# Second cross attention of a decoder: the next sequence's keys go ahead of a step's scores

## The chip, the cores and the metric

The kernel runs on one core of a Trainium2 chip. The metric is the device time of one execution in microseconds (us), as a median over runs. The engines are TensorE (PE for matmuls, PEld for its weight loads), VectorE (DVE), ScalarE (ACT), GpSimd (POOL) and SyncE (SP), which here issues DMAs. Each engine works through its own instructions in order; semaphores tie the engines together.

## The reference, cut to what matters

The kernel computes a whole decoder of two layers on 16 sequences of 100 rows and 256 columns: retention, a cross attention, a mixture of experts, a Mamba block, a second cross attention and a product in int8, each with a residual and a layer norm. The change is in the second cross attention, which has 16 heads of 64 columns and a context of 361 rows and 192 columns for each sequence:

```python
q = (x @ Wq).reshape(B, Nq, h, dh)
k = (context @ Wk).reshape(B, Nk, h, dh)
v = (context @ Wv).reshape(B, Nk, h, dh)
scores = jnp.einsum('bqhd,bkhd->bhqk', q, k) * scale
attn = jax.nn.softmax(scores, axis=-1)
out = jnp.einsum('bhqk,bkhd->bqhd', attn, v).reshape(B, Nq, h * dh)
return out @ Wo + bo
```

All data are float32 but the int8 product at the end, which is done in bf16.

## The kernel before, in words

The second cross attention is `cross1`, and its loop is `attend`, which serves nothing else. The order of TensorE, ScalarE and VectorE in it is the order in which the code is written (`manual_schedule`); POOL and SP are left to the framework. The work goes in steps, numbered n from 0. Step n belongs to sequence b = n // 4 and to four of its 16 heads, quad = n % 4. There are 64 such steps and two more that only end the pipeline. A step has these parts:

- `scores(b, quad)`: four matmuls (L1656, each over 64 rows, two heads side by side on the array) into two tiles `sc`; two maxima on VectorE (L1661, tile `top`); four exponentials on ScalarE (L1666), each with its sum, into `s` and `den`.
- `prepare(b + 1, quad)`: for the next sequence, a list of one or two pieces. The first, `keys`, makes two key tiles: two matmuls over 128 rows of the context (L591) and two over the remaining 64 (L593, side by side), and two copies on VectorE (L1620, tile `k`). The second, `sources`, makes a third of the values in the same way (L591, L593, copies at L1637, tile `v`). It is missing at quad 0. At quad 0 `prepare` also issues the load of the context on SP (L581). The last sequence has nothing to prepare, so the list is empty in steps 60 to 63.
- `values(b', quad')` for the step two earlier (`depth` is 2): first the transposes of the weights' first two column blocks (L600), with the copies to `pT` by VectorE for the first block and by ScalarE for the second (L603); then, as its second piece, the transposes of the third block, its copy by ScalarE, twelve products with the values (L1695) and a copy to `oT` by ScalarE (L1701).
- `weigh`: the reciprocal of the sums on VectorE (L1674) and a multiplication of the four heads' weights by it on POOL (L1675).
- After the last quad of a sequence `finish`: the output projection (L155) and a row sum on VectorE (L1712). After quad 2 of every fourth sequence `queries` for the next four. `later` holds the pieces of the layer norm (means with a square root on ScalarE, L192; normalization, L200) and of the int8 product (L1785 to L1839), one or a few at the end of certain steps.

PSUM holds three tags of tiles with two buffers each: `sc` for scores (two banks a tile), `mm` for keys, values and the projections, `tr` for transposes and the products. A step with all its parts takes four tiles of `tr`: the two first transposes, the third, and the products, so the third waits for VectorE's copy of the first, and the products wait for ScalarE's copy of the second.

Of the kernel before, what the change touches and what calls it, by code (L numbers as in the profile page):

```python
# [90 lines left out]
class Net:  # L91
# [452 lines left out]
    def attend(self, scores, prepare, values, finish, queries, weigh, depth, later):  # L544

        n_quads = 4 * B
        engines = {mybir.EngineType.PE, mybir.EngineType.Activation, mybir.EngineType.DVE}  # L550
        with self.tc.manual_schedule(engines=engines):
            queries(0)
            for part in range(4):
                for step in prepare(0, part):
                    step()
            for n in range(max(n_quads + depth, max(later) + 1)):
                b, quad = divmod(n, 4)
                ahead, behind = [], []
                if n < n_quads:
                    scores(b, quad)  # L560
                    if b + 1 < B:
                        ahead = prepare(b + 1, quad)
                if depth <= n < n_quads + depth:
                    behind = values(*divmod(n - depth, 4))
                for i in range(max(len(ahead), len(behind))):
                    for steps in (ahead, behind):
                        if i < len(steps):
                            steps[i]()
                if n < n_quads:
                    weigh(b, quad)  # L570
                if n < n_quads and quad == 2 and b % G == G - 1 and b + 1 < B:
                    queries(b // G + 1)
                if depth <= n < n_quads + depth and (n - depth) % 4 == 3:
                    finish((n - depth) // 4)
                for step in later.get(n, []):
                    step()
# [1448 lines left out]
```

## Time and profile before

| what | value |
|---|---|
| time, median of 3 runs | 2023.19 us (2020.81 to 2028.84) |
| the profiled execution's own time | 2028.71 us |
| its span, first to last instruction | 2026.5 us |
| busy TensorE, share of the span | 1815.4 us, 90% |
| busy VectorE | 1134.7 us, 56% |
| busy ScalarE | 975.7 us, 48% |
| busy POOL | 683.5 us, 34% |
| mean granted TensorE clock | 0.942 of full speed |
| the first scores of the second cross attention | 1333.8 us |
| the first scores of step 60, the first without keys | 1957.65 us |

The profile is of one execution. Its rows give an instruction's start, its duration, the line that issued it and the tiles that it writes and reads; "idle before" names the time that the engine had nothing to run and what ended it. The granted clock is given by window: 1.00 is full speed, 0.50 is half. A group of matmuls in float32 shows two records for each matmul. The steps of the loop are told apart by their scores (L1656).

### The profile page before, as it was taken

Reading aid. Unit: us, or ns where it says so; the run is one execution under the profiler, and the core shown is the slowest. Engines: PE = TensorE matmul, PEld = TensorE weight load, DVE = VectorE, ACT = ScalarE, POOL = GpSimd, SP = SyncE. Lnnn points to the kernel's source line nnn. Section 1 sums busy time; section 2 is a strip of 40 time slices with the busy share of each in tenths; the row PEclk is TensorE's granted clock in tenths of the full one; section 3 lists DMA queues with packets and bytes.
Section 4 is the critical chain, followed back from the end, with each engine's and each line's share of the span. In section 5 each row is a group of like instructions: output and inputs, shape, how many; then the busy total and the mean of one; then the engine's idle time right before and its main releaser. Section 6 shows DMA issues by size and latency. Waiting matters only on the chain. (4 is left out here: it accounts for less than half of the span.)

```text
span 2026.5 us, 31942 instructions
## 1 busy us (share of the span) xinstructions
PE 1815.4 (90%) x12268; PEld 1071.4 (53%) x12268; DVE 1134.7 (56%) x2466; ACT 975.7 (48%) x2293; POOL 683.5 (34%) x501
## 2 busy tenths in 40 slices
PE   6998899999949996789898898999999999999985
PEld 3566556556535664455455455545555555555554
DVE  2454576767742222687888867444436545444654
ACT  4553376666622221487676676423334434344343
POOL 1322232334330001457557566422222322322231
PEclk8999999989869998899898899999999999999996
DMA  4700600001023111422111111000000000000000
GB/s 133 320 1 1 213 30 24 27 22 40 3 96 131 45 45 38 129 92 77 42 43 60 40 51 46 20 15 9 8 8 8 16 16 8 8 16 9 8 9 8
DMA packets 46848, 96.98 MB, mean 48 GB/s; under 512 B 5844, under 2 KB 25940, under 8 KB 44266
## 3 DMA queue, kind: packets, MB, share of 16 engines
q1 hardware_dynamic: 41642, 83.75, 12.3%
q0 software_dynamic: 5056, 11.20, 1.8%
q8 instruction: 98, 1.61, 0.3%
q14 instruction: 52, 0.43, 0.1%
HBM read 69.48 MB, written 25.44 MB: 47 GB/s over the span
## 5 line engine op out<-in xcount | busy, mean ns | idle before, releaser
L1675 POOL TENSOR_TENSOR s<-s,den 100x1444 f32<-100x1444 f32 x64 | 166.1, 2595 | 506.3 <-DVE den L1674 465.7
L155 PE MATMUL mm<-xT,w_mamba_in 128*128 128x400 f32 x512 | 206.7, 548 | 28.6 <-ACT sz L1353 22.7
L1666 ACT ACTIVATE s<-sc,top 100x361 f32<-100x361 f32 x256 | 140.4, 561 | 182.5 <-DVE top L1661 174.6
L603 ACT COPY pT<-tr 128x400 f32<-128x400 f32 (+1 forms) x192 | 94.1, 494 | 187.7 <-PE tr L600 185.9
L1204 DVE SCALAR_TENSOR_TENSOR xc<-mm,pv,xc 128x388 f32<-128x388 f32 (+2 forms) x192 | 119.9, 625 | 76.7 <-ACT xc L1199 69.2
L737 POOL TENSOR_SCALAR w_experts<-w_experts 100x1444 f32<-100x1444 f32 x64 | 89.0, 1390 | 217.8 <-DVE w_experts L733 171.5
L155 PEld LDWEIGHTS mm<-xT,w_mamba_in 128*128 128x128 f32 x512 | 101.2, 207 | 115.1 <-ACT sz L1353 30.6
L745 ACT ACTIVATE w_experts<-w_experts,top 100x361 f32<-100x361 f32 x256 | 149.3, 586 | 22.5 <-POOL w_experts L737 22.4
L1661 DVE TENSOR_REDUCE top<-sc 100x2 f32<-100x722 f32 x128 | 110.1, 901 | 87.0 <-PE sc L1656 87.0
L603 DVE COPY pT<-tr 128x400 f32<-128x400 f32 x192 | 105.4, 568 | 58.3 <-PE tr L600 51.4
L733 DVE TENSOR_SCALAR_CACHE_REDUCE w_experts<-sc 100x361 f32<-100x361 f32 x256 | 121.2, 530 | 16.2 <-PE sc L727 15.6
L600 PEld LDWEIGHTS tr<-cn,s 100*128 100x128 f32 (+1 forms) x768 | 76.1, 154 | 87.2 <-issue 63.9
L1637 DVE COPY v<-mm 128x512 f32<-128x512 f32 (+1 forms) x96 | 61.9, 686 | 107.3 <-PE mm L593 107.3
L155 PE MATMUL sc<-w_experts,e_xT 128*128 x256 | 117.1, 601 | 2.1 <-DMA e_x<-rows 2.1
L1387 POOL TENSOR_TENSOR y<-y,sz 128x400 f32<-128x400 f32 x64 | 66.5, 1040 | 145.1 <-DVE y L1384 112.3
L600 PE MATMUL tr<-cn,s 100*128 100x100 f32 (+1 forms) x768 | 99.3, 267 | 17.2 <-DVE pT L603 17.0
L600 PE MATMUL tr<-cn,w_experts 100*128 100x100 f32 (+1 forms) x768 | 97.8, 267 | 13.7 <-ACT w_experts L745 6.6
L1695 PE MATMUL tr<-pT,v 128*64 128x100 f32 (+1 forms) x1536 | 98.2, 268 | 12.1 <-ACT pT L603 7.3
L1324 POOL TENSOR_TENSOR L<-L,cols 100x800 f32<-100x800 f32 x64 | 100.0, 1563 | 23.6 <-DMA L<-sums 23.5
L1407 PE MATMUL acc<-y,w_mamba_out 128*128 128x400 f32 x256 | 102.3, 523 | 3.7 <-ACT w_mamba_out L1414 1.9
L1620 DVE COPY k<-mm 128x361 f32<-128x361 f32 x128 | 62.3, 529 | 68.1 <-PE mm L593 68.1
L591 PE MATMUL mm<-ctx,x_wk 128*128 128x361 f32 x256 | 95.3, 494 | 2.2 <-DVE v L1637 1.6
(298 smaller groups left out, 3647.5 us busy)
## 6 DMA issues: line engine op xcount, KB each, us to landing
L<-sums SPq DMA_DIRECT2D x64, 312.5 KB
rows<-nothing SPq DMA_DIRECT2D x15, 1024.0 KB
w_experts<-in_moe_w_dram SPq DMA_DIRECT2D x24, 512.0 KB
ctx<-in_ctxT_dram SPq DMA_DIRECT2D x32, 361.0 KB
e_x<-rows SPq DMA_DIRECT2D x32, 128.0 KB
rows<-e_y SPq DMA_DIRECT2D x32, 128.0 KB
w_mamba_in<-in_m_w_in_dram SPq DMA_DIRECT2D x1, 2048.0 KB
w_mamba_in<-in_m_w_in_dram POOLq DMA_DIRECT2D x1, 2048.0 KB
```

The lines of the kernel that those rows point to most:

```text
L155: self.nc.tensor.matmul(out, lhsT, rhs, start=i == 0, stop=i == len(pairs) - 1)
L600: self.nc.tensor.transpose(pt[:n, h * T : (h + 1) * T], probs[:, h, k0 : k0 + n], self.ident(T))
L603: evict(pT[:n, k, :], pt[:n, :GT])
L733: nc.vector.tensor_scalar(s[:, h, :], sc[h // 2][:T, h % 2, :CTX], -1e4, 1e4, ALU.max, ALU.min, accum_out=top[:, h : h + 1],)
L745: nc.scalar.activation(s[:, h, :], s[:, h, :], AF.Exp, bias=top[:, h : h + 1], scale=-1.0, accum_out=dens[b][:, hd : hd + 1],)
L1204: nc.vector.scalar_tensor_tensor(a3[:, :, s:], p3[:, :, : T - s], w(k), a3[:, :, s:], ALU.mult, ALU.add)
L1324: nc.gpsimd.tensor_tensor(ls[n], ls[n], bc(c, 3, T), ALU.subtract)
L1407: nc.tensor.matmul(acc[:, c, :GT], self.w_out[:, i, c * P : (c + 1) * P], y, start=i == 0, stop=i == 15)
L1661: nc.vector.tensor_reduce(top[:, 2 * p : 2 * p + 2], sc[p][:T, :, :CTX], AX.X, ALU.max, negate=True)
L1666: nc.scalar.activation(s[:, h, :], sc[h // 2][:T, h % 2, :CTX], AF.Exp, bias=top[:, h : h + 1], accum_out=den[:, h : h + 1],)
L1675: nc.gpsimd.tensor_tensor(s, s, bc(den, 2, CTX), ALU.mult)
L1695: nc.tensor.matmul(po[64 * jj : 64 * jj + 64, i * T : (i + 1) * T], v[k][:n, (4 * quad + h) * 64 : (4 * quad + h + 1) * 64], pT[:n, k, h * ...
```

## The change

In a step of `attend`, the first piece of `prepare` (the keys of the next sequence) is taken from its list and issued ahead of the scores. In the loop that interleaves what is left, the pieces of `values` are now named before those of `prepare`. A step thus runs: keys, scores, first transposes, values, then third transposes and products; before it ran: scores, keys, first transposes, values, third transposes and products.

```diff
                 b, quad = divmod(n, 4)
                 ahead, behind = [], []
                 if n < n_quads:
-                    scores(b, quad)
                     if b + 1 < B:
                         ahead = prepare(b + 1, quad)
+                        ahead.pop(0)()
+                    scores(b, quad)
                 if depth <= n < n_quads + depth:
                     behind = values(*divmod(n - depth, 4))
                 for i in range(max(len(ahead), len(behind))):
-                    for steps in (ahead, behind):
+                    for steps in (behind, ahead):
                         if i < len(steps):
                             steps[i]()
```

## The prediction

> **What bounds the kernel now.** I read the page first, then the waits of the second cross attention (1333 us to the end), then the timeline of single steps, then TensorE's busy time and granted clock in short windows.
>
> ```profile
> span 2026.5 us, 31942 instructions
> ...
> PE 1815.4 (90%) x12268; PEld 1071.4 (53%) x12268; DVE 1134.7 (56%) x2466; ACT 975.7 (48%) x2293; POOL 683.5 (34%) x501
> ...
> PEclk8999999989869998899898899999999999999996
> ```
>
> TensorE is the bound; in the stage concerned, slices 27 to 39, its clock is nearly whole. The waits of that stage (us in total, times, longest) leave little on TensorE itself:
>
> ```profile
> PE tr L600 <- DVE pT L603: 17.0, 18, 1.8
> ...
> PE tr L1695 <- ACT pT L603: 7.3, 6, 2.3
> ```
>
> The stage makes 64 steps, numbered n from 0; n mod 4 = 0 begins a sequence and has keys but no values ("short step"). A short step, n = 32 (columns: start, busy, engine, line):
>
> ```profile
> 1666.43 1.46 PE L1656 MATMUL sc<-k,q 64*100 64x361 f32 x8
> ...
> 1667.83 1.48 PE L591 MATMUL mm<-ctx,x_wk 128*128 128x361 f32 x4
> ...
> 1670.05 0.91 PE L600 MATMUL tr<-cn,s 100*128 100x100 f32 x8
> 1670.14 0.98 DVE L1620 COPY k<-mm 128x361 f32<-128x361 f32 x2 [1.08 <-PE mm L593]
> ...
> 1671.04 0.56 DVE L603 COPY pT<-tr 128x400 f32<-128x400 f32 x1
> 1671.04 0.49 ACT L603 COPY pT<-tr 128x400 f32<-128x400 f32 x1 [0.42 <-PE tr L600]
> ...
> 1671.65 0.61 PE L600 MATMUL tr<-cn,s 100*105 100x100 f32 x4 [0.70 <-DVE pT L603]
> ...
> 1673.69 1.46 PE L1656 MATMUL sc<-k,q 64*100 64x361 f32 x8
> ```
>
> It lasts 7.26 us, with 0.70 idle. The keys stand between the scores and the transposes, so the maxima and the exponentials run under them, and ScalarE is free when the transposes come. A step with values (n = 31, 1657.16 to 1666.43) lasts 9.27 without a gap on TensorE.
>
> **The change part by part.** It adds and removes no instruction. On ScalarE, POOL and SP the order stays exactly as it is, the context loads included (one is issued at 1664.54 and first used at 1705, so moving its call ahead of the scores changes nothing). On TensorE and VectorE, in steps 0 to 59, keys come before scores and key copies before the maxima. Transposes stood before values already. Steps 60 to 63 have no keys and stay.
>
> *One switch less.* Keys end with two 64-row matmuls (L593), scores are 64-row too. At the start of step 2 the trace has 64-row products running straight into scores:
>
> ```profile
> 1344.05 1.13 PE L593 MATMUL mm<-x_wv,ctx 64*128 64x512 f32 x4
> 1345.01 1.38 PE L1656 MATMUL sc<-k,q 64*100 64x361 f32 x8
> ```
>
> From L593 to the next group is 0.96 here and 1.06 where transposes follow (1641.98 to 1643.04). The scores take 1.31 here (keys follow at 1346.32) and 1.39 behind 128-row products (1657.16 to 1658.55). So 0.18 is saved wherever scores come to stand behind keys and TensorE is the bound: steps 3 to 59 less 14 short ones, 43 x 0.18 = -7.7 us.
>
> *The short steps lose their cover.* Scores now run straight into transposes. The nearest row is step 62, where before has that order:
>
> ```profile
> 1978.71 1.73 DVE L1661 TENSOR_REDUCE top<-sc 100x2 f32<-100x722 f32 x2 [0.37 <-PE sc L1656]
> ...
> 1979.71 0.56 ACT L1666 ACTIVATE s<-sc,top 100x361 f32<-100x361 f32 x1 [5.77 <-DVE top L1661]
> ...
> 1980.35 0.57 DVE L603 COPY pT<-tr 128x400 f32<-128x400 f32 x1
> ...
> 1980.97 0.61 PE L600 MATMUL tr<-cn,s 100*105 100x100 f32 x4 [0.87 <-DVE pT L603]
> ...
> 1981.87 0.90 ACT L603 COPY pT<-tr 128x400 f32<-128x400 f32 x2
> ...
> 1982.43 1.31 PE L1695 MATMUL tr<-pT,v 128*64 128x100 f32 x24 [0.85 <-ACT pT L603]
> ```
>
> Queued behind the exponentials on ScalarE is the second transpose's copy, and the products need the bank that it frees. Count from the start of the keys. Key copies start at 2.31 (1670.14 - 1667.83) and take 0.90: VectorE is free at 3.21. Maxima 1.64 (1980.35 - 1978.71): copy pT at 4.85; third transposes 0.62 later, 5.47. Exponentials start 1.00 behind the first maximum, 4.21; 2.16 later (1981.87 - 1979.71) the other pT copy, 6.37; products 0.56 later, 6.93; the next step 1.24 later (1983.67 - 1982.43), 8.17. Against 7.26 that is +0.91. The early copies of the keys don't help, since the maxima wait behind them. Steps 4, 8, 12, 16, 32, 48: 6 x 0.91. Steps 24, 40, 56 end with int8 products and save one switch: 3 x 0.73. Steps 20, 36, 52 already wait 1.83 behind a normalization: about 3 x 0.3. In 28 and 44 an ACT_TABLE_LOAD (1.28) comes ahead of the exponentials: products 8.21, end 9.45 against 7.68, 2 x 1.77. Sum +12.1.
>
> *Steps with values* hide the same chain: transposes 3.43, values 4.17, products 7.60, with the copy ready at 6.93, 0.67 to spare. A table load eats it in 19, 35, 51 (about +0.4 each). Keys that follow int8 products (25, 26 and likewise) wait for the second bank until two L1832 (0.88 together) are done: 6 x 0.43. The row sum behind `finish` (0.42) ends as the second key matmul wants its bank, paid by a switch saved there. Values that waited for key copies in before no longer do: -1. Filling the pipe in steps 0 to 2: +0.8. With small switches: +2.3. Where the trace is silent on these, I bound them by 0 and +5.
>
> Without the clock: -7.7 + 12.1 + 2.3 = +6.7 us.
>
> *The clock.* Windows of 3.41 us (columns after the window: length, PE, PEld, DVE, ACT, POOL busy, PEclk, DMA):
>
> ```profile
> 1708.65:1712.06 3.41, 1.58 (x14) 1.16 (x12) 3.11 (x7) 2.65 (x9) 0.00 (x0) 1.00 0.00 0
> 1712.06:1715.48 3.42, 3.42 (x30) 2.67 (x30) 3.32 (x5) 0.83 (x3) 2.60 (x1) 0.50 0.00 0
> 1879.33:1882.74 3.41, 2.22 (x14) 1.02 (x12) 3.41 (x8) 1.50 (x5) 0.00 (x0) 1.00 0.00 0
> 1882.74:1886.15 3.41, 2.72 (x34) 2.00 (x36) 3.08 (x5) 1.99 (x7) 2.20 (x1) 1.00 0.00 0
> ```
>
> Idle 1.83 of a window, and the next ran at half clock; idle 1.19, and it did not. In this stage drops followed 1.47 and more, none 1.31 and less: I take 1.4. The new short step has gaps of 1.13 and 0.84 (4.34 to 5.47, 6.09 to 6.93), 1.98 together. A window must start between 2.94 and 4.92 to hold 1.4 of it: 1.98/3.41 = 58%. Nine plain steps 5.2 drops, three at about 74% 2.2, two always: 9.4, less the 2 of before (after steps 20 and 36) = 7.4. One drop costs 1.1: steps 20 and 21 together take 22.92, 36 and 37 22.62, but 52 and 53, without a drop, 21.68. +8.1 us.
>
> Here a rule speaks otherwise. The Trainium skill, "TensorE: Matmul & The Clock Gate", Part 1, has the clock fall only after a whole idle window of about 3.4 us. By it no gap here counts, and the sum stays +6.7; by the rows it is +14.8. The rows decide.
>
> The sum stands on the profiled execution (2028.71 us, span 2026.5), which lies 5.5 above the median of the runs; I add it to the median: 2023.2 + 14.8 = 2038.0.
>
> **The rivals.** About 0.5%, 10 us, is what a measurement of this kernel can tell from no change.
> - *The clock stays up* (not slower): decided in the window that holds both gaps; if it takes more than 1.98 idle, or the gaps fall into two windows (as in step 62, which had no drop), only +6.7: 2029.9. For: step 62. Against: step 61, with gaps of 0.67 and 0.85, dropped. Chance 0.23.
> - *No switch is saved*, 128-column keys before 100-column scores costing as much as 128 rows do: +22.5, 2045.7. Against: the rows at 1344. Chance 0.13.
> - *ScalarE is late in steps with values too*: above 0.67 of added delay each 0.2 costs 9 us; about 2050. Chance 0.05.
> - *Faster*: copies come early enough that also the 0.70 of 14 short steps goes, -7.7 - 9.8: 2006. The chain above speaks against it. Chance 0.06.
>
> **How the numbers follow.** The main case has 0.53, its own range 2033 to 2043, a tenth of it under 10 us. Slower: 0.48 + 0.13 + 0.05 = 0.66. Same: 0.05 + 0.23 + 0.02 (from the last rival) = 0.30. Faster 0.04. The range 2027 to 2048 holds the main case, the first rival and most of the second.
>
> **What would show it.** Right: short steps of about 8.2 us with two waits, on DVE pT and on ACT pT, at L600 and L1695 (together near 30 us more than before); value steps of 9.09; some seven more windows at half clock, starting within the products of short steps. Wrong: value steps still 9.27 (no switch saved), or waits in them before L1695; short steps at 7.3 or less; a clock that stays whole.

## The result, and the profile after

The changed kernel takes 2042.47 us (median of 5 runs, 2040.11 to 2053.88) against 2023.35 before (5 runs, 2020.81 to 2028.84). The ratio over all runs is 1.0104 with a 95% interval from 1.0080 to 1.0127 (that of the two medians alone is 1.0094): slower by 16 to 26 us. The prediction had 2038.0 with a range from 2027 to 2048 and gave "slower" 0.66.

From the page after, the span, TensorE's busy time and the granted clock:

```profile
span 2038.1 us, 31942 instructions
...
PE 1806.9 (89%) x12268; PEld 1079.5 (53%) x12268; DVE 1132.4 (56%) x2466; ACT 969.1 (48%) x2293; POOL 682.5 (33%) x501
...
PEclk9999999999869997999998999999999999999996
```

The instructions are as many as before. TensorE's busy time over the whole span is 8.5 us less, but that lies ahead of the changed stage. The stage is looked at from the start of step 0 to that of step 60; the first row is before, the second after (length, busy time of PE, PEld, DVE, ACT and POOL, granted clock, and two figures for DMA):

```profile
1333.77:1957.65 623.88, 603.06 (x3815) 329.04 (x3811) 312.70 (x586) 243.75 (x708) 165.17 (x65) 0.99 0.04 11
1326.40:1969.34 642.94, 603.90 (x3813) 342.13 (x3813) 309.93 (x585) 237.75 (x708) 165.02 (x65) 0.97 0.04 10
```

The stage is 19.1 us longer. TensorE's busy time in it is nearly the same and its idle time 18.2 us more. This doesn't make waiting the whole cause: the changed order saves TensorE busy time, and a lower clock adds some, as is shown below. (All line numbers from 560 on are one higher than before: L1656 is now L1657, L600 is L601, L603 is L604, L1695 is L1696.) The waits from 1326 us on (us in total, times, longest):

```profile
PE tr L1696 <- ACT pT L604: 22.2, 21, 2.3
PE tr L601 <- DVE pT L604: 21.1, 18, 1.6
```

Before, the two stood at 7.3 and 17.0: 19.0 us more. The wait for ScalarE's copy, which six instances had before, now comes in 21. The short step n = 32, whole:

```profile
1666.41 1.48 PE L592 MATMUL mm<-ctx,x_wk 128*128 128x361 f32 x4
...
1667.82 0.88 PE L594 MATMUL mm<-ctx,x_wk 64*128 64x361 f32 x4
1668.53 1.38 PE L1657 MATMUL sc<-k,q 64*100 64x361 f32 x8
1668.73 0.97 DVE L1621 COPY k<-mm 128x361 f32<-128x361 f32 x2 [2.88 <-PE mm L594]
1669.62 1.72 DVE L1662 TENSOR_REDUCE top<-sc 100x2 f32<-100x722 f32 x2
1669.84 0.91 PE L601 MATMUL tr<-cn,s 100*128 100x100 f32 x8
1670.61 0.56 ACT L1667 ACTIVATE s<-sc,top 100x361 f32<-100x361 f32 x1 [3.76 <-DVE top L1662]
...
1671.25 0.56 DVE L604 COPY pT<-tr 128x400 f32<-128x400 f32 x1
...
1671.87 0.61 PE L601 MATMUL tr<-cn,s 100*105 100x100 f32 x4 [1.12 <-DVE pT L604]
...
1672.78 0.90 ACT L604 COPY pT<-tr 128x400 f32<-128x400 f32 x2
...
1673.33 1.31 PE L1696 MATMUL tr<-pT,v 128*64 128x100 f32 x24 [0.85 <-ACT pT L604]
1674.57 0.88 PE L592 MATMUL mm<-ctx,x_wk 128*128 128x361 f32 x2
```

Keys, scores and transposes follow each other without a gap, then TensorE waits twice: 1.12 us for VectorE, which first copied the keys and then made the maxima, and 0.85 us for ScalarE, which is still at the exponentials when the second transpose wants its copy. The step takes 8.16 us; it took 7.26. A step with values, n = 3, has no gap and shows the other side of the change:

```profile
1348.00 0.88 PE L594 MATMUL mm<-ctx,x_wk 64*128 64x361 f32 x4
1348.71 1.38 PE L1657 MATMUL sc<-k,q 64*100 64x361 f32 x8
1350.02 0.91 PE L601 MATMUL tr<-cn,s 100*128 100x100 f32 x8
```

The same groups of step 3 in before:

```profile
1354.24 1.46 PE L1656 MATMUL sc<-k,q 64*100 64x361 f32 x8
1355.63 1.48 PE L591 MATMUL mm<-ctx,x_wk 128*128 128x361 f32 x4
1357.04 0.88 PE L593 MATMUL mm<-ctx,x_wk 64*128 64x361 f32 x4
1357.85 0.91 PE L600 MATMUL tr<-cn,s 100*128 100x100 f32 x8
```

From the start of the keys' second part to that of the next group it is 0.71 now, with scores next, and was 0.81, with transposes next. From the start of the scores to the next group it is 1.31 and was 1.39. The whole step is 9.07 us; it was 9.27.

The third effect is in the clock. In these traces the clock changes only at whole multiples of 3.41 us from each other. Windows cut at these times (columns as above), the first pair from step 28 on, the second in step 32:

```profile
1617.80:1621.21 3.41, 1.28 (x18) 1.09 (x20) 1.07 (x3) 3.05 (x10) 0.76 (x1) 1.00 0.00 0
1621.21:1624.63 3.42, 3.42 (x19) 1.92 (x14) 2.96 (x4) 0.33 (x1) 1.84 (x1) 0.50 0.02 5
1669.00:1672.42 3.42, 2.30 (x19) 1.34 (x15) 2.82 (x5) 1.81 (x7) 0.00 (x0) 1.00 0.00 0
1672.42:1675.83 3.41, 2.56 (x29) 1.76 (x28) 0.18 (x1) 1.58 (x5) 2.51 (x1) 1.00 0.00 0
```

In step 28 both gaps fell into one window, TensorE was idle for 2.13 of it, and the next window ran at half clock. In step 32 the two gaps, 1.12 and 0.85, fell into different windows, and the clock stayed. In steps 0 to 60 there were 11 such drops with 12 half-clock windows; before had 2. That the spans differ by only 11.6 has another reason, shown by the last experiment.

### The profile page after: what moved, and what is told of

Read it like the earlier page. It is cut to its first block, busy times and chain, and to the rows that moved or that the text cites. A ratio compares the mean times of both kernels' runs of the same rounds, so it can differ in the third digit from the quotient of the medians.

```text
span 2038.1 us, 31942 instructions
## 1 busy us (share of the span) xinstructions
PE 1806.9 (89%) x12268; PEld 1079.5 (53%) x12268; DVE 1132.4 (56%) x2466; ACT 969.1 (48%) x2293; POOL 682.5 (33%) x501
## 5 line engine op out<-in xcount | busy, mean ns | idle before, releaser
L604 DVE COPY pT<-tr 128x400 f32<-128x400 f32 x192 | 105.3, 569 | 54.4 <-PE tr L601 46.7
L604 ACT COPY pT<-tr 128x400 f32<-128x400 f32 (+1 forms) x192 | 93.0, 499 | 81.2 <-PE tr L601 79.9
L1696 PE MATMUL tr<-pT,v 128*64 128x100 f32 (+1 forms) x1536 | 102.5, 281 | 25.8 <-ACT pT L604 22.2
L601 PEld LDWEIGHTS tr<-cn,s 100*128 100x128 f32 (+1 forms) x768 | 76.2, 154 | 92.5 <-issue 64.5
L601 PE MATMUL tr<-cn,s 100*128 100x100 f32 (+1 forms) x768 | 99.4, 267 | 21.3 <-DVE pT L604 21.1
L592 PE MATMUL mm<-ctx,x_wk 128*128 128x361 f32 x256 | 105.6, 530 | 4.5 <-DVE v L1638 3.1
L601 PE MATMUL tr<-cn,w_experts 100*128 100x100 f32 (+1 forms) x768 | 97.2, 267 | 13.8 <-ACT w_experts L746 6.1
```

The costliest lines, as they stand in the source:

```text
L592: self.nc.tensor.matmul(out, lhsT, rhs, start=True, stop=False)
L601: self.nc.tensor.transpose(pt[:n, h * T : (h + 1) * T], probs[:, h, k0 : k0 + n], self.ident(T))
L604: evict(pT[:n, k, :], pt[:n, :GT])
L1696: nc.tensor.matmul(po[64 * jj : 64 * jj + 64, i * T : (i + 1) * T], v[k][:n, (4 * quad + h) * 64 : (4 * quad + h + 1) * 64], pT[:n, k, h * ...
```

## The experiments

Theory: three effects, switches of row tiling (between groups over 128 rows of the array and groups over 64) saved in steps with values, cover lost in short steps (n mod 4 = 0), and a clock that falls because of the gaps. The rivals are that the order costs or gains alike in every kind of step, and that the clock has nothing to do with the gaps. "Steps 0 to 60" is always the time from the start of step 0 to that of step 60, 623.88 us in the profile of before shown above.

**Keys ahead in steps with values only, and in short steps only.**

```diff
-                    if b + 1 < B:
-                        ahead = prepare(b + 1, quad)
-                        ahead.pop(0)()
+                    ahead = prepare(b + 1, quad) if b + 1 < B else []
+                    first = quad > 0        # the other kernel: quad == 0
+                    if ahead and first:
+                        ahead.pop(0)()
                     scores(b, quad)
+                    if ahead and not first:
+                        ahead.pop(0)()
```

> Keys go ahead of the scores only in steps with values (n mod 4 > 0); short steps (n mod 4 = 0) keep the old order. Theory (two effects of opposite sign: a switch of row tiling saved in value steps, cover lost in short steps): value steps 9.07 us instead of 9.27, short steps 7.26 again, windows at half clock between steps 0 and 60 back to about 2; steps 0 to 60 about 5 us shorter than before (ratio about 0.9975). Rival (keys ahead of scores cost time wherever they stand): value steps no shorter and the ratio over 1.000.

> Keys go ahead of the scores only in the short steps. Theory: the whole loss sits there. Short steps 8.2 to 9.9 us, value steps 9.27 as before, about 11 windows at half clock; steps 0 to 60 about 22 to 25 us longer than before, so somewhat more than the changed kernel's 19.1 (ratio 1.011 to 1.013). Rival (loss spread over all steps): less than half of 19 us.

Measured: value steps alone 2012.37 us, ratio 0.9938 (0.9926 to 0.9950); steps 0 to 60 615.9 us, 8 shorter (10.5 shorter than in the second profile of before, at the end of this section). Value steps without other work take 9.07, short ones 7.26, and there are two half-clock windows. Short steps alone 2048.76 us, ratio 1.0130 (1.0113 to 1.0147); steps 0 to 60 650.4 us, 26.5 longer, with value steps at 9.27, undisturbed short ones at 8.16 and 11 half-clock windows. So the change is two changes: one half of it is a gain of about 0.6%, the other a loss of 1.3%, and the kernel as changed shows what is left. In the stage the two make -8.0 + 26.5 = 18.5, against 19.1. Both came out above what was expected: the gain was 8 for 5, the loss 26.5 for 22 to 25.

**TensorE kept busy in the gaps.**

```diff
+            short = quad == 2 and b < B - 2      # the values' side of a short step
+
+            def fill(cols):
+                if short:
+                    idle = self.ps("mm")
+                    nc.tensor.matmul(idle[:, :cols], wk[:, :P], wv[:, :cols], start=True, stop=True)
+
             def transposes(ks):
                 ...
+                fill(512 if 0 in ks else 361)
```

> The changed kernel, and in each of the 14 short steps two more matmuls whose result nobody reads, one of 512 columns behind the first transposes and one of 361 behind the third ones, so that TensorE is busy in the two waits. Theory (the waits leave a window idle for over 1.4 us, and the next runs at half clock): windows at half clock between steps 0 and 60 fall from 11 to 4 or less, plain short steps 8.2 to 8.4, steps 0 to 60 about 7 to 10 us longer than before instead of 19 (ratio 1.004 to 1.005). Rival (the clock falls for another reason, or costs nothing by itself): still about 11 windows, or a ratio of 1.010 or more since the extra matmuls only add work.

Measured: 2024.14 us, ratio 1.0004 (0.9995 to 1.0013). The stage and its short step n = 32 (L1690 is the filling):

```profile
1326.44:1951.77 625.33, 606.87 (x3869) 336.63 (x3869) 309.32 (x585) 237.46 (x708) 165.03 (x65) 1.00 0.04 11
```

```profile
1662.32 0.91 PE L601 MATMUL tr<-cn,s 100*128 100x100 f32 x8
1663.06 1.05 PE L1690 MATMUL mm<-x_wv,x_wk 128*128 128x512 f32 x2
1664.35 0.61 PE L601 MATMUL tr<-cn,s 100*105 100x100 f32 x4 [0.24 <-DVE pT L604]
1664.79 0.80 PE L1690 MATMUL mm<-x_wv,x_wk 128*128 128x361 f32 x2
1665.80 1.31 PE L1704 MATMUL tr<-pT,v 128*64 128x100 f32 x24 [0.21 <-ACT pT L604]
```

The granted clock of the stage is 1.00, with no window at half speed, and the 28 useless matmuls make it 17.6 us shorter than the changed kernel (642.94 against 625.33). The short step still takes 8.16 us, since the products come when ScalarE's copy does; only the clock is different. So the gaps cause the drops, and a window at half clock costs 17.6 / 12 = 1.47 us. The gain was above what was expected, because both the number of windows saved and their price had been set too low.

**What makes the scores start sooner.**

```diff
-        for out, (lhsT, rhs) in zip(outs, wide):
-            self.nc.tensor.matmul(out, lhsT, rhs, start=True, stop=False)
-        for out, (lhsT, rhs) in zip(outs, halves):
-            self.nc.tensor.matmul(out, lhsT, rhs, start=False, stop=True)
+        for n, pairs in enumerate((halves, wide) if halves_first else (wide, halves)):
+            for out, (lhsT, rhs) in zip(outs, pairs):
+                self.nc.tensor.matmul(out, lhsT, rhs, start=n == 0, stop=n == 1)
```

`halves_first` is set for the keys alone.

> The changed kernel, with the two parts of the keys exchanged: the two matmuls over the remaining 64 rows first, then the two over 128 rows. The order keys, scores, transposes stays; only the neighbour of the scores is now a 128-row matmul. Theory (value steps gain because 64-row keys run into 64-row scores without a switch): value steps such as 3, 11, 27, 43 and 59 go from 9.07 back to about 9.25. Rival (the gain comes from the order of keys and scores as such, by way of the copies that are ready earlier): they stay at 9.07.

Measured: steps 3, 11, 27, 43 and 59 take 9.25 us each. The scores of step 3:

```profile
1350.68 1.46 PE L1657 MATMUL sc<-k,q 64*100 64x361 f32 x8
1352.07 0.91 PE L600 MATMUL tr<-cn,s 100*128 100x100 f32 x8
```

They last 1.39 again with a 128-row neighbour, in the same order of keys and scores. The order of keys and scores is still the new one, so the gain is that of neighbours with the same row tiling. (This is one run, of 2057.91 us. It is longer for a further reason: the keys now begin with matmuls that want both `mm` banks, and behind an output projection the second of them waits for the row sum that frees its bank. Such steps take 9.86 instead of 9.18.)

**All three copies of a short step by VectorE**, in the changed kernel.

```diff
-                    self.probs_transposed(s, pT, k, nc.scalar.copy if k else nc.vector.tensor_copy)
+                    on_act = k > 0 and not (quad == 2 and b < B - 2)
+                    self.probs_transposed(s, pT, k, nc.scalar.copy if on_act else nc.vector.tensor_copy)
```

> The changed kernel; in the 14 short steps all three copies of transposes are made by VectorE, so that none of them queues behind the exponentials on ScalarE. Theory (of the two waits of a short step the second, at the products, is ScalarE's queue; the first, at the third transposes, is VectorE's and stays): the first wait stays at about 1.1 us, the second shrinks from 0.84 to about 0.4, plain short steps 7.6 to 7.8 us instead of 8.16, fewer windows at half clock; 5 to 12 us shorter than the changed kernel (ratio against before 1.004 to 1.008). Rival (the products wait for something else, the scores' bank or the weights): short steps stay near 8.2 and the ratio near 1.010.

Measured: 2018.26 us, ratio 0.9977 (0.9968 to 0.9987). Its short step n = 32 takes 7.58 us:

```profile
1660.48 1.04 DVE L604 COPY pT<-tr 128x400 f32<-128x400 f32 x2
...
1661.10 0.61 PE L601 MATMUL tr<-cn,s 100*105 100x100 f32 x4 [1.12 <-DVE pT L604]
...
1661.64 0.56 PE L1697 MATMUL tr<-pT,v 128*64 128x100 f32 x8
1661.75 0.57 DVE L604 COPY pT<-tr 105x400 f32<-105x400 f32 x1 [0.23 <-PE tr L601]
...
1662.37 0.91 PE L1697 MATMUL tr<-pT,v 105*64 105x100 f32 x16 [0.17 <-DVE pT L604]
```

The first wait is the same to the hundredth, the wait on ScalarE is gone, and a wait of 0.17 on VectorE has come: the second wait was ScalarE's queue. With smaller gaps the drops fall to 5, of one window each. The gain over the changed kernel, 19.2 us in steps 0 to 60, is more than was expected. By the price of 1.47 the seven windows less make 10.3 of it, an estimate; the rest is the shorter waits.

**A better version.** Two kernels keep the keys ahead in steps with values only, and also exchange the copies of the first two transposes between VectorE and ScalarE. One does this in all short steps, the other only in the nine that neither follow a normalization nor have a table load. The exchange in the second:

```diff
+                    swap = quad == 2 and b in (0, 1, 2, 3, 5, 7, 9, 11, 13)
+                    on_act = k != 1 if swap else k > 0
-                    self.probs_transposed(s, pT, k, nc.scalar.copy if k else nc.vector.tensor_copy)
+                    self.probs_transposed(s, pT, k, nc.scalar.copy if on_act else nc.vector.tensor_copy)
```

> As the kernel with keys ahead only in steps with values, and in the 14 short steps the copies of the first two transposes change engines: ScalarE, which is idle there, takes the first and VectorE, which is behind the key copies, the second. Theory: the third transposes no longer wait for VectorE; short steps 6.75 us instead of 7.26, 14 x 0.5 = 7 us more saved, steps 0 to 60 about 12 us shorter than before (ratio 0.994). Rival (the copy by ScalarE comes as late as VectorE's, or the products then wait for VectorE): short steps 7.2 and no gain over the kernel with keys ahead in value steps.

> Keys ahead only in steps with values, and the exchange of the first two copies between ScalarE and VectorE only in the nine short steps that neither follow a normalization (20, 36, 52) nor have a table load (28, 44). Theory: those nine short steps take 6.85 us instead of 7.26, the other five stay as with the old copies; steps 0 to 60 about 11 to 12 us shorter than before, and 3.7 shorter than with keys ahead in value steps alone (ratio about 0.992). Rival (ScalarE's and VectorE's copies only trade places, and a drop of the clock takes the gain): ratio no better than 0.994.

Measured: in all short steps 2009.14 us, ratio 0.9935 (0.9917 to 0.9953), no measurable gain over value steps alone. That the ratio is the one expected is luck: steps 0 to 60 are about 9 us shorter than before (615.0), where 12 were expected. Plain short steps fell to 6.84 us, but steps 20, 36 and 52 rose from 8.47, 8.05 and 8.01 to 9.71, 8.59 and 8.93 (step 20 partly at half clock): there VectorE is late with a normalization, so the maxima are late, so the exponentials on ScalarE are, and the copy that was given to ScalarE stands behind them. The third transposes of step 52 with value steps alone, and with the exchange:

```profile
1869.69 0.61 PE L604 MATMUL tr<-cn,s 100*105 100x100 f32 x4 [1.46 <-DVE pT L607]
1866.77 0.61 PE L604 MATMUL tr<-cn,s 100*105 100x100 f32 x4 [2.04 <-ACT pT L607]
```

In 28 and 44 ScalarE is late with a table load, the third transposes wait 0.70 for VectorE as without the exchange, and nothing is gained (7.67 in both). In nine short steps 2005.21 us, ratio 0.9909 (0.9892 to 0.9925): the fastest of all, 0.9% below before. Its short step n = 32:

```profile
1654.68 0.49 ACT L607 COPY pT<-tr 128x400 f32<-128x400 f32 x1
1655.02 0.57 DVE L607 COPY pT<-tr 128x400 f32<-128x400 f32 x1
1655.22 0.61 PE L604 MATMUL tr<-cn,s 100*105 100x100 f32 x4 [0.29 <-ACT pT L607]
```

ScalarE, free at this point, makes the copy while VectorE still copies keys, and the wait of 0.70 is down to 0.29. Steps 0 to 60 take 611.8 us, 12.1 less than before, as expected.

**Before, profiled again.**

> The kernel before, profiled a second time, to see how much of a difference between two profiles lies outside the changed stage. If the first profile of before was long in its first part by chance of the clock windows: its second cross attention starts at 1324 to 1328 us as in all later profiles, not at 1333.8, and its steps 0 to 60 take 622 to 626 us again. If not: it starts near 1334 again, and the earlier stages of the other kernels would be faster for a reason that the change doesn't explain.

Measured: span 2020.8 us; the second cross attention starts at 1325.5 us, and steps 0 to 60 take 626.5 us, with 4 drops. So the first profile of before was 8 us long in the stages ahead (it has 56 half-clock windows there, this one 47), which hides 7.4 us of the difference between the spans of before and after (after starts the stage at 1326.4). Within the changed stage the two profiles of before differ by 2.6 us, with two drops more in the second; the change costs 16.5 to 19.1 there.

## Why the prediction was right, and where not

- *One switch less*: the main value steps were to go from 9.27 to 9.09. They take 9.07, and the exchange of the keys' parts put them back to 9.25. The mechanism is right. Counted by groups, what is saved is one whole stretch of 64-row work: before, scores and the keys' second part were two such stretches in a step, and now they are one (the values' second part is one of its own in both). So two changes of tiling are gone, and the prediction's two differences, 0.10 and 0.08, belong to these.
- *Short steps*: right. The chain gave 8.17; undisturbed ones (16, 32) take 8.16. The filled kernel, which has no clock drop, shows the others: with a table load 9.45 was predicted and 9.43 measured, after a normalization 8.68 and 8.67, with int8 products 8.55 and 8.59. The sum of +12.1 stands against +11.2 there, or +11.9 with the slow clock that before had in its step 36 taken out. The two waits named are right too, at 1.13 and 0.84 against 1.12 and 0.85.
- *The waits in total*, "near 30 us more": too high, 19.0 were measured. The two new waits of 14 short steps do make 27.6 by the prediction's own figures, but the 0.70 that each of these steps had before, 9.8 in all, goes. What is left is 17.8.
- *Steps with values hide the chain*: right; they show no wait before their products except after a table load (step 19: 9.44, as predicted within 0.1).
- *The small terms*, +2.3: too high, they come to about nothing. In the filled kernel the value steps make -9.5 and the first three steps -0.3; 1.4 of this is the slow clock of before in steps 21 and 37, which leaves -8.3. The 43 value steps account for -7.7 at 0.18 each, or -8.6 at the 0.20 measured, so between -0.6 and +0.3 remains. Two parts were mis-sized. Filling the pipe cost nothing. And the values' wait for key copies was worth more than 1 us: steps 29, 45 and 53 took 0.26, 0.26 and 0.38 more than step 13 (12.93) in before, and in the filled kernel all four take 12.64, as do 21 and 37. With these two put like 53 that is 1.7 us.
- *The clock*: the right mechanism, mis-sized. 7.4 more drops at 1.1 us made 8.1; there were 11 against 2 (or 4 in the second profile of before), one of them two windows long, at 1.47 a window or 1.60 a drop. Part of the fault in the 1.1 can be seen in before. Step 53, taken as undisturbed, has a wait for the key copies: its values start 1.06 us behind the first transposes. In steps 21 and 37, behind a slow window, they start 0.74 behind. The slow windows thus took up 0.3 us of waiting each, and their price seemed that much smaller. In the changed kernel values start 0.74 to 0.75 behind the transposes in every value step from step 5 on, so there is no such wait to take up. Against the first profile of before the term came to about 15.5 us: 17.6 from the filled kernel, less about 2.1 for the drops of before.
- *The rule of the Trainium skill* ("TensorE: Matmul & The Clock Gate", Part 1, table of the two states), by which the clock falls after a whole idle window, would have left +6.7 and "same". The windows above and the filled kernel decide against it here: in the stage drops came after windows with 1.4 to 2.5 us idle, none of them idle throughout. The prediction told only half of that part, which also has a kernel whose clock swings because TensorE "micro-idles between MM groups frequently enough"; that is nearer to what was measured.
- *Sum*: 14.8 predicted in the stage, 16.5 to 19.1 measured. Two errors, the clock too low by about 7 and the small terms too high by about 3, offset each other in part. That the time came so close to 2038 owes something to this, so to luck. The direction does not: it rested on the clock. With no slow windows in either kernel the stage is only 3.6 us longer (the filled kernel's 625.3, against 623.9 less 2.1 for before), where the prediction had 6.7.
- *The rivals*: "the clock stays up" is refuted by the 11 drops, "no switch is saved" by the value steps, "ScalarE late in value steps" by the missing waits, "faster" by the short steps.

## What to carry to other kernels

Before an instruction group is moved, ask what it covered, that is, which work of other engines ran under it. The keys between scores and transposes gave VectorE and ScalarE 2.2 us. In steps that have another cover, the values, the keys could be moved at a gain; in steps without one they could not. So apply a change of order by kind of step. A gap on TensorE can cost twice, once itself and once in the clock of what follows, so add up the gaps that can fall into one clock window.

## What the runs showed of the hardware

The granted clock fell to half for the next 3.41 us after windows in which TensorE was idle for a part of the time only. Counted over steps 0 to 60 in all ten profiles, 42 windows at full clock had 1.37 us idle or more (2.54 at most), and 39 of them were followed by one at half. Of those with 1.23 to 1.36 idle, 4 of 18 were; of those with 1.19 or less, none. The three that were borne had 1.49 and 1.56 (filled kernel) and 1.69 (keys' parts exchanged), so idle time alone does not set the edge; what else counts is not shown. A window that was already at half needed less: with 0.38 us idle or more another one at half followed (7 times), with 0.31 or less the full clock came back (43 times). Useless matmuls in the gaps made a kernel 17.6 us faster in the stage than the same kernel without them.

Neighbours in the queue matter to TensorE without any wait. In step 3 the pairs of 64-row matmuls follow each other every 0.30 us, across the border of two such groups too. From the last pair to a group over 128 rows it is 0.39 to 0.40, and from the first pair behind such a group to the second 0.38 to 0.41. Taking one stretch of 64-row work out of a step, with its entry and its end, was worth 0.18 to 0.20 us.
